# The adjacency in two tiles, p through DRAM by POOL's queue, and the scalings on ScalarE: a two-layer graph attention kernel on one core

## The chip, the cores and the metric

The kernel runs on one core of one Trainium2 chip. The metric is the device time of one execution in microseconds (us), the median of several runs. A core has five engines with an instruction stream each: TensorE (PE in the profile; PEld is its weight load), VectorE (DVE), ScalarE (ACT), GpSimd (POOL) and SyncE (SP). SP, ACT and POOL also issue DMA transfers, and each issues in its own order: an issue that waits holds up everything behind it on that engine. Instructions of one engine run in the order in which they were written; engines wait for each other by semaphores.

## The reference

There are 16 graphs of 1024 nodes with 256 features, x (16, 1024, 256), and an integer adjacency adj (16, 1024, 1024). In the data that the kernel is timed on, adj holds only 0 and 1 and is symmetric in its making.

```
# layer 0
e0    = leaky((h * a0) @ h.T)                  # slope 0.2; e1..e3 likewise for adj 2..4
alpha = sigmoid(where(adj == 1, e0, ..., -inf))
x1    = layernorm(x + alpha @ h + bias)
# layer 1
H  = x1 @ W;  s = H @ a_src;  d = H @ a_dst
e  = where(adj != 0, exp(-leaky(s[:, None] + d[None, :])), 0)
y  = elu((e @ H) / rowsum(e))
out = layernorm(x1 + y)
```

## The kernel before

All of it is float32 on the chip, except adj, which is kept as bfloat16. `one_kind_pass` computes everything for an adjacency of one kind (0 and 1); flags (`check_adj`, `check_pq`) collect whether that held, and only if one is raised `general_pass` runs afterwards. With this data it doesn't run.

P = 128, so a graph has NT = 8 blocks of 128 nodes, and HT = 4 blocks are a half. Each graph b passes through three stages, in which TensorE works almost without a gap. Stages of neighbouring graphs are interleaved by an order that is written out by hand in the loop `for b in range(1, B)`:

- **Strips of b** (lines 480 to 498). `strip(b, jt)` computes the scores of block jt with the blocks from jt on (they are symmetric, so only the upper triangle is computed): matmuls (L198), two tanh on ScalarE (L206, L207), the larger of both on VectorE (L208). The sigmoid is 0.5 (1 + tanh(z/2)). The scores lie in one of four `tb` tiles, so strip jt can be written only when strip jt-4 has been sent out. `finish` (L214) adds 1 and multiplies by adj, and POOL adds the identity, twice, to the diagonal block (L224), which puts the residual x into the sum. `dump` (L230, L234) turns the strip in blocks of 32 and sends it to DRAM by four DMAs, `gather` (L238) brings it back as the lower triangle, and `mask` (L244) multiplies that by adj. `project(b-1, t)` of the graph before runs between: matmuls of x1 with W and two further columns (L343), two exponentials into w and pq, and H scaled by w (L351 to L353). Since exp(-leaky(s+d)) is factored, layer 1 needs p, one number for each node, as a row on all 128 partitions. `spread_p` makes it at the stage's end: TensorE transposes each block's column, broadcast to 128 columns (L362, 8 per graph), and ScalarE copies the result from PSUM (L363).
- **Sum 0 of b** (lines 507 to 522): for each block t, `sum0` runs 8 matmuls (L294), VectorE takes the result with the bias (L302) and its mean and variance (L264, L265), and after four blocks POOL computes 1/sqrt of the variance (`rstd`, L271 to L279). `scale0` applies both on VectorE (L283). Beside it run the last masks, `weights(b-1, t)` (L375: the smaller of p times q and 1, masked by adj, 128x1024 at a time), `scale1` and the store of graph b-2, and on ScalarE `check_adj`, a square with a sum over 128x2048 of adj (L116).
- **Sum 1 of b-1** (lines 527 to 558): 8 times 8 matmuls of e with H and a column of ones (L382), `elu` (L397 to L403), `add` (L408, L409, mean and variance), and the preparation of the next graph: x1 goes to DRAM and comes back with its blocks of 32 turned (`save_x1`, `fetch_x1`, `turn_x1`, L320, L110, L331), and x of the next graph is loaded in the same form (`load_blocks`, `turn_x`).

The first graph has its own order (lines 439 to 470), with `mirror` (L252, L253) in place of dump, gather and mask; `make_Wx` prepares the further columns of W there, and x of graph 1 is loaded by ScalarE's DMA queue (line 451). The last graph has its own end (lines 561 to 599), in which the first three blocks of sum 1 run together, step by step with the weights.

adj of a graph is one tile [128, 8, 1024] with two buffers. [...]

Of the kernel before, what the change touches and what calls it, by code (L numbers as in the profile page):

```python
# [18 lines left out]
P = 128  # L19
# [10 lines left out]
def one_kind_pass(  # L30
# [60 lines left out]
    def load_adj(b, by_columns=False):  # L91
        adjs[b] = two.tile([P, NT, N], BF16, tag="adj", name=f"adj_{b}")
        rows = adjT[b].rearrange("(t p) i -> p t i", p=P)
        for h in range(2):
            for g in range(2):
                if by_columns:
                    v = (slice(None), ts(g, HT), ts(h, HALF))
                elif g == 0:
                    v = (slice(None), ts(h, HT))
                else:  # L100
                    continue
                nc.gpsimd.dma_start(adjs[b][v], rows[v])

    def load_blocks(dst, src, n0, n, queue=nc.sync):


        v = src[ds(n0, n), :].rearrange("(nb nn) (c q dd) -> q c nn nb dd", nn=SQ, c=ND, dd=SQ)
        for c in range(ND):
            for q in range(P // SQ):
                queue.dma_start(  # L110
                    dst[ts(q, SQ), c, ds(n0, n)].rearrange("p (nb dd) -> p nb dd", dd=SQ), v[q, c]
                )

    def check_adj(b, n):
        junk = one.tile([P, NT // CHECKS, N], BF16, tag="tmp", name=f"junk_{b}_{n}")
        nc.scalar.activation(  # L116
            junk,
            adjs[b][:, ts(n, NT // CHECKS), :],
# [20 lines left out]
    load_adj(0, by_columns=True)  # L139
    load_adj(1)  # L140
# [4 lines left out]
    a_bc = one.tile([P, 2 * D], F32, tag="p", name="a_bc")  # L145
# [64 lines left out]
    def finish(b, jt, c0=0, c1=N):  # L210
# [7 lines left out]
            adjs[b][:, jt, c0:c1],  # L218
# [23 lines left out]
    def mask(b, t):  # L242
        v = als[b][:, t + 1 :, ts(t, P)]
        nc.vector.scalar_tensor_tensor(v, v, 1.0, adjs[b][:, t + 1 :, ts(t, P)], ALU.add, ALU.mult)  # L244

    def mirror(b, t):

        for j0 in range(t + 1, NT, HT):
            n = min(HT, NT - j0)
            pt = ps_t.tile([P, HT, P], F32, tag="t", name=f"pal_{b}_{t}_{j0}")  # L250
            for q in range(n):
                nc.tensor.transpose(pt[:, q, :], tbs[b, t][:, ts(j0 + q - t, P)], ident)  # L252
            nc.vector.scalar_tensor_tensor(  # L253
                als[b][:, ds(j0, n), ts(t, P)],
                pt[:, 0:n, :],
                1.0,
                adjs[b][:, ds(j0, n), ts(t, P)],
                ALU.add,
                ALU.mult,
            )  # L260
# [21 lines left out]
    def scale(y, mv, r):  # L282
        nc.vector.tensor_scalar(y, y, mv[:, 0:1], r, ALU.subtract, ALU.mult)  # L283
# [3 lines left out]
    def sum0(b, t):  # L287
        if t == 0:
            x1s[b] = two.tile([P, NT, D], F32, tag="x1", name=f"x1_{b}")
            mv0s[b] = small.tile([P, NT, 2], F32, tag="mv0", name=f"mv0_{b}")  # L290
            r0s[b] = {}
# [12 lines left out]
        if t % HT == HT - 1:  # L304
            g = t // HT
            r0s[b][g] = rstd(mv0s[b][:, ts(g, HT), :], f"0_{b}_{g}")

    def scale0(b, t):
        scale(x1s[b][:, t, :], mv0s[b][:, t, :], r0s[b][t // HT][:, t % HT : t % HT + 1])
# [23 lines left out]
    def project(b, t):  # L333

        if t == 0:
            if b < B - 1:
                Hs[b] = one.tile([P, NT, D + 1], F32, tag="H", name=f"H_{b}")
            else:
                Hs[b] = two.tile([P, NT, D + 1], F32, tag="adj", name=f"H_{b}")
# [10 lines left out]
        w = Hs[b][:, t, D : D + 1]  # L350
        nc.scalar.activation(w, pt[:, 1:2], AF.Exp, scale=-SLOPE)  # L351
        nc.scalar.activation(pqs[b][:, t, :], pt[:, 0:2], AF.Exp, scale=SLOPE - 1.0)
        nc.scalar.mul(Hs[b][:, t, 0:D], pt[:, 2:], w)  # L353

    def spread_p(b, g):
# [7 lines left out]
        nc.scalar.copy(p_bcs[b][:, ts(g, HALF)], pt.rearrange("p t q -> p (t q)"))  # L363

# [6 lines left out]
    def weights(b, m):  # L371

        if m == 0:
            es[b] = one.tile([P, NT, N], F32, tag="ew" if b < B - 1 else "al", name=f"e_{b}")
        nc.vector.scalar_tensor_tensor(  # L375
            es[b][:, m, :], p_bcs[b], pqs[b][:, m, 1:2], adjs[b][:, m, :], ALU.mult, ALU.min
        )

    hs, ys, mv1s, r1s, rms = {}, {}, {}, {}, {}

    def sum1(b, t, acc, m):
# [3 lines left out]
            rhs=Hs[b][:, m, :],  # L385
# [26 lines left out]
    def center(b, t0, n):  # L412

        mv = mv1s[b][:, ds(t0, n), :]
        r = rstd(mv, f"1_{b}_{t0}")
        mr = small.tile([P, NT], F32, tag="mr", name=f"mr_{b}_{t0}")[:, 0:n]
        nc.gpsimd.tensor_tensor(mr, mv[:, :, 0], r, ALU.mult)
        nc.gpsimd.tensor_scalar(mr, mr, -1.0, None, ALU.mult)
        for t in range(n):
            rms[b, t0 + t] = r[:, t : t + 1], mr[:, t : t + 1]  # L420

    def scale1_act(b, t):
# [568 lines left out]
```

## Time and profile before

| | us |
|---|---|
| time, median of 3 runs (lowest to highest) | 1329.43 (1328.62 to 1329.67) |
| the profiled execution: its own time | 1330.3 |
| its span in the profile | 1328.4 |
| busy in the span: PE, DVE, ACT, POOL | 1280.3, 1019.5, 546.5, 243.4 |
| sum 0 stage of a graph, as a rule | 27.64 |
| sum 1 stage of a graph, as a rule | 27.84 |
| strips stage of graphs 2 to 15 | 23.54 to 27.39 |

In the groups of the profile a line gives engine and operation, the tiles written and read, the count, the busy time, the mean duration in ns, and the idle time of the engine just before these instructions with what ended it. In the table of waits each line is "engine line <- what it waited for: us in total, times, longest". In the timeline the columns are start, duration, engine, line, operation, and in brackets the idle time before. In the table of windows, an engine's busy time in the window is followed by its count of instructions; PEclk, DMA share and GB/s follow at the end.

### The profile page before, as it was taken

What the parts mean: (1) busy time and instruction counts of PE and PEld (TensorE: products, weight loads), DVE (VectorE), ACT (ScalarE), POOL (GpSimd) and SP (SyncE); (2) the same over time, 40 slices, a digit from 0 to 9 for tenths busy, and PEclk for the clock granted to TensorE, in tenths of its full rate; (3) what the DMA queues carried; (4) which work ended last, traced back from release to release, by engine and by line L of the source; (5) the groups of instructions that cost most, each with busy time, mean ns of one, the idle gap of its engine ahead of it and who ended that gap; (6) DMA issues with size and microseconds to landing.
All of it is one profiled execution on the core that took longest, in us unless ns stands there. A gap on an engine that the chain in (4) does not pass through costs nothing.

```text
span 1328.4 us, 17516 instructions
## 1 busy us (share of the span) xinstructions
PE 1280.3 (96%) x5550; PEld 1037.4 (78%) x5550; DVE 1019.5 (77%) x2318; ACT 546.5 (41%) x1236; POOL 243.4 (18%) x486
## 2 busy tenths in 40 slices
PE   7879999999999999999999999999999999999995
PEld 5758788687887878788687887878778687787874
DVE  5576886968869687886878869687886878869764
ACT  3352452715336162452715336162451624427034
POOL 2111111211112122111211112122111211112113
PEclk9999999999999999999999999999999999999998
DMA  9265687575677756687575677856686565775211
GB/s 215 54 133 113 109 174 143 113 164 104 145 141 157 160 103 150 109 180 143 111 162 106 150 138 152 162 105 151 111 177 130 110 151 106 172 143 111 68 29 66
DMA packets 606516, 173.36 MB, mean 130 GB/s; under 512 B 485584, under 2 KB 590928, under 8 KB 606416
## 3 DMA queue, kind: packets, MB, share of 16 engines
q1 hardware_dynamic: 580144, 137.56, 48.0%
q0 software_dynamic: 17952, 33.56, 14.8%
q10 hardware_dynamic: 8320, 1.05, 0.5%
q8 instruction: 46, 0.75, 0.2%
q14 instruction: 54, 0.44, 0.1%
HBM read 144.57 MB, written 61.08 MB: 155 GB/s over the span
## 4 chain that ended last, share of the span: by engine, by line
PE 83%; DVE 6%; DMA 3%; ACT 3%; SPq 2%; ACTq 1%; issue 1%; POOL 0%; DVEq 0%; POOLq 0%
PE acc L294 32%; PE acc L382 32%; PE pe L198 13%; PE pH L343 5%; DMA mir<-tb 2%; SPq L234 2%; DVE tb L208 1%; DVE al L214 1%; ACTq L110 1%; DVE tb L230 1%; ACT tb L206 1%; PE pp L362 1%; ACT low L207 1%; DVE st L264 1%; DVE y L409 0%
## 5 line engine op out<-in xcount | busy, mean ns | idle before, releaser
L382 PE MATMUL acc<-H,e 128*128 128x257 f32 x2048 | 448.7, 380 | 1.6 <-DVE e L375 1.6
L294 PE MATMUL acc<-x,al 128*128 128x256 f32 x2048 | 448.5, 381 | 0.0
L382 PEld LDWEIGHTS acc<-H,e 128*128 128x128 f32 x2048 | 387.9, 190 | 59.5 <-DVE e L375 2.4
L294 PEld LDWEIGHTS acc<-x,al 128*128 128x128 f32 x2048 | 389.5, 191 | 53.5 <-issue 0.5
L402 ACT ACTIVATE h<-acc,rinv 128x256 f32<-128x256 f32 x128 | 60.2, 470 | 562.2 <-DVE rinv L400 559.3
L198 PE MATMUL pe<-xa,xT 128*128 128x384 f32 (+3 forms) x768 | 269.4, 488 | 0.2 <-ACT low L207 0.2
L198 PEld LDWEIGHTS pe<-xa,xT 128*128 128x128 f32 x768 | 143.3, 191 | 87.5 <-issue 42.6
L271 POOL TENSOR_SCALAR ve<-mv 128x4 f32<-128x4 f32 (+3 forms) x51 | 18.0, 352 | 811.4 <-DVE mv L265 796.7
L375 DVE SCALAR_TENSOR_TENSOR e<-p,pq,adj 128x1024 f32<-128x1024 f32 x128 | 162.8, 1275 | 2.8 <-ACT p L363 2.8
L206 ACT ACTIVATE tb<-pe 128x512 f32<-128x512 f32 (+1 forms) x192 | 94.3, 491 | 136.5 <-PE pe L198 87.2
L343 PE MATMUL pH<-Wx,x1T 128*128 128x258 f32 x512 | 133.0, 386 | 7.1 <-DVE x1T L331 4.2
L343 PEld LDWEIGHTS pH<-Wx,x1T 128*128 128x128 f32 x512 | 97.2, 193 | 43.0 <-issue 17.6
L116 ACT ACTIVATE junk<-adj,minus 128x2048 bf16<-128x2048 bf16 x64 | 128.4, 2007 | 1.5
L397 DVE COPY rs<-acc 128x1 f32<-128x1 f32 x128 | 19.7, 154 | 138.9 <-PE acc L382 138.5
L208 DVE TENSOR_TENSOR tb<-tb,low 128x512 f32<-128x512 f32 (+1 forms) x192 | 99.3, 542 | 28.4 <-ACT low L207 25.8
L224 POOL TENSOR_TENSOR al<-ident,al 128x128 f32<-128x128 f32 x128 | 68.9, 538 | 240.9 <-DVE al L214 240.9
L214 DVE SCALAR_TENSOR_TENSOR al<-tb,adj 128x512 f32<-128x512 f32 (+7 forms) x132 | 99.4, 753 | 4.1
L302 DVE SCALAR_TENSOR_TENSOR x<-acc,bias_bc 128x256 f32<-128x256 f32 x128 | 54.3, 424 | 60.4 <-PE acc L294 59.2
L207 ACT ACTIVATE low<-pe 128x512 f32<-128x512 f32 (+1 forms) x192 | 93.3, 486 | 3.6 <-DVE tb L208 3.5
L273 POOL TENSOR_TENSOR r<-ve,power 128x4 f32<-128x4 f32 (+3 forms) x51 | 78.5, 1539 | 4.3
L230 DVE STREAM_TRANSPOSE tb<-tb 128x896 f32<-128x896 f32 (+6 forms) x105 | 74.7, 712 | 3.6
L244 DVE SCALAR_TENSOR_TENSOR al<-al,adj 128x896 f32<-128x896 f32 (+6 forms) x105 | 72.9, 694 | 0.9 <-DMA al<-mir 0.7
(58 smaller groups left out, 866.3 us busy)
## 6 DMA issues: line engine op xcount, KB each, us to landing
adj<-in_adjT POOLq DMA_DIRECT2D x30, 1024.0 KB, 13.6
x_rows<-x SPq DMA_DIRECT2D x32, 512.0 KB, 3.7
x1T<-x_rows SPq DMA_DIRECT2D x256, 64.0 KB, 2.4
x<-in_x SPq DMA_DIRECT2D x15, 1024.0 KB, 6.2
out<-y SPq DMA_DIRECT2D x30, 512.0 KB, 3.0
xT<-in_x SPq DMA_DIRECT2D x112, 128.0 KB, 3.2
mir<-tb SPq DMA_DIRECT2D x60, 112.0 KB, 2.4
al<-mir SPq DMA_DIRECT2D x15, 448.0 KB, 4.1
```

The source lines that it names most:

```text
L116: nc.scalar.activation(junk, adjs[b][:, ts(n, NT // CHECKS), :], AF.Square, bias=minus1, scale=2.0, accum_out=chk[:, b * CHECKS + n : b * ...
L198: nc.tensor.matmul(pe[:, 0:w], lhsT=xTs[b][:, c, ts(jt, P)], rhs=xas[b][:, c, ds(jt * P + o, w)], start=(c == 0), stop=(c == ND - 1),)
L206: nc.scalar.activation(tb[:, ds(o, w)], pe[:, 0:w], AF.Tanh, scale=0.5)
L207: nc.scalar.activation(low[:, 0:w], pe[:, 0:w], AF.Tanh, scale=0.5 * SLOPE)
L208: nc.vector.tensor_tensor(tb[:, ds(o, w)], tb[:, ds(o, w)], low[:, 0:w], ALU.max)
L214: nc.vector.scalar_tensor_tensor(als[b][:, jt, c0:c1], tbs[b, jt][:, c0 - jt * P : c1 - jt * P], 1.0, adjs[b][:, jt, c0:c1], ALU.add, ALU. ...
L230: nc.vector.transpose(tb, tb)
L273: nc.gpsimd.tensor_tensor(r, ve, power[:, 0:n_t], ALU.pow)
L294: nc.tensor.matmul(acc, lhsT=als[b][:, jt, ts(t, P)], rhs=xs[b][:, jt, :], start=(jt == 0), stop=(jt == NT - 1),)
L343: nc.tensor.matmul(pt, lhsT=x1Ts[b][:, c, ts(t, P)], rhs=Wx[:, c, :], start=(c == 0), stop=(c == ND - 1),)
L375: nc.vector.scalar_tensor_tensor(es[b][:, m, :], p_bcs[b], pqs[b][:, m, 1:2], adjs[b][:, m, :], ALU.mult, ALU.min)
L382: nc.tensor.matmul(acc, lhsT=es[b][:, m, ts(t, P)], rhs=Hs[b][:, m, :], start=(m == 0), stop=(m == NT - 1),)
```

## The change

- adj of a graph becomes two tiles of four row blocks each (`adj0`, `adj1`, two buffers each). The first half of graph b+1 is loaded at t = 5 of the sum 0 stage, when the weights of blocks 0 to 3 have been made, the second after the stage. Instructions on adj that cross the border of the halves are split in two (`adj_rows`).
- p: TensorE transposes the eight columns at once to 8 rows, ScalarE copies 8x128, POOL's queue writes that to DRAM and reads it back to all 128 partitions (`share_p`). This is issued at the strips' step 6 (step 7 for the first graph) and no longer at the stage's end; the projections come earlier in the stage. The weights are made from t = 2 of sum 0 on, not from t = 0. The last graph keeps `spread_p`.
- `scale0` and `scale1` run on ScalarE, from factors that POOL makes (`center`).
- The first graph: `make_Wx` after the first four strips; x of graph 1 by SP's queue; `check_adj(0, t)` at t = 0 to 3 rather than 4 to 7. Graph 1's strips get another order for x1 of graph 0.
- The end: weights of block 2 before the loop over m, and in the last loop the elu of a block stands before the add of the block before it.

```diff
+    def load_adj(b, g, columns=None):
+        if (b, g) not in adjs:
+            adjs[b, g] = two.tile([P, HT, N], BF16, tag=f"adj{g}", name=f"adj_{b}_{g}")
+        columns = columns or slice(None)
+        rows = adjT[b].rearrange("(t p) i -> p t i", p=P)[:, ts(g, HT), columns]
+        nc.gpsimd.dma_start(adjs[b, g][:, :, columns], rows)
+
+    def adj_rows(b, j0, j1, columns):
+        for g in range(2):
+            k0, k1 = max(j0, g * HT), min(j1, (g + 1) * HT)
+            if k0 < k1:
+                yield slice(k0, k1), adjs[b, g][:, k0 - g * HT : k1 - g * HT, columns]
...
     def mask(b, t):
-        v = als[b][:, t + 1 :, ts(t, P)]
-        nc.vector.scalar_tensor_tensor(v, v, 1.0, adjs[b][:, t + 1 :, ts(t, P)], ALU.add, ALU.mult)
+        for js, rows in adj_rows(b, t + 1, NT, ts(t, P)):
+            v = als[b][:, js, ts(t, P)]
+            nc.vector.scalar_tensor_tensor(v, v, 1.0, rows, ALU.add, ALU.mult)
...
-    def scale(y, mv, r):
-        nc.vector.tensor_scalar(y, y, mv[:, 0:1], r, ALU.subtract, ALU.mult)
+    def center(mv, what):
+        r = rstd(mv, what)
+        n = mv.shape[1]
+        mr = small.tile([P, NT], F32, tag="mr", name=f"mr_{what}")[:, 0:n]
+        nc.gpsimd.tensor_tensor(mr, mv[:, :, 0], r, ALU.mult)
+        nc.gpsimd.tensor_scalar(mr, mr, -1.0, None, ALU.mult)
+        return [(r[:, t : t + 1], mr[:, t : t + 1]) for t in range(n)]
+
+    def scale(y, r, mr):
+        nc.scalar.activation(y, y, AF.Identity, bias=mr, scale=r)
...
+    def share_p(b):
+        pt = ps_t.tile([P, HT, P], F32, tag="t", name=f"prow_{b}")[0:NT, 0, :]
+        nc.tensor.transpose(pt, pqs[b][:, :, 0], ident)
+        row = small.tile([NT, P], F32, tag="row", name=f"row_{b}")
+        nc.scalar.copy(row, pt)
+        p_row = dram.tile([N], F32, tag="p_row", name=f"p_row_{b}")
+        nc.gpsimd.dma_start(p_row.rearrange("(t p) -> t p", p=P), row)
+        p_bcs[b] = one.tile([P, N], F32, tag="p", name=f"p_{b}")
+        nc.gpsimd.dma_start(p_bcs[b], p_row.partition_broadcast(P))
...
-    make_Wx()
     strip(0, 0)
...
+    make_Wx()
     load_x(1)
     new_xT(1)
-    load_blocks(xTs[1], x[1], 0, N, nc.scalar)
+    load_blocks(xTs[1], x[1], 0, N)
...
-        if t >= NT - CHECKS:
-            check_adj(0, t - NT + CHECKS)
+        if t < CHECKS:
+            check_adj(0, t)
...
-        projects = [[jt] for jt in range(NT)]
+        projects = [[0, 1], [2], [3], [4, 5], [6], [7], [], []]
         if prev == 0:
-            projects = [[], [], [], [0, 1], [2, 3], [], [4, 5], [6, 7]]
+            projects = [[], [], [], [], [0, 1], [2, 3], [], [4, 5, 6, 7]]
...
-            if prev == 0 and jt in (1, 2):
-                scale0(0, 2 * jt + 2)
-                scale0(0, 2 * jt + 3)
-            if prev == 0 and jt == 2:
+            if prev == 0 and jt == 1:
+                for t in range(HT, NT):
+                    scale0(0, t)
                 save_x1(0, 1)
-                fetch_x1(0, 1)
-            if prev == 0 and jt in (2, 5):
-                turn_x1(0, (jt - 2) // 3)
             finish(b, jt)
             if jt < NT - 1:
                 dump(b, jt)
+            if prev == 0 and jt == 1:
+                fetch_x1(0, 1)
+            if prev == 0 and jt in (3, 6):
+                turn_x1(0, (jt - 3) // 3)
             if jt >= 1:
                 gather(b, jt - 1)
             for t in projects[jt]:
                 project(prev, t)
+            if jt == (6 if prev > 0 else 7):
+                share_p(prev)
             if jt >= 5:
                 mask(b, jt - 5)
-        for g in range(2):
-            spread_p(prev, g)
...
-            weights(prev, t)
+            for m in ([], [], [0, 1], [2], [3], [4], [5], [6, 7])[t]:
+                weights(prev, m)
...
             sum0(b, t)
+            if t == 5 and not last:
+                load_adj(b + 1, 0)
...
         if not last:
-            load_adj(b + 1)
+            load_adj(b + 1, 1)
...
     for m in range(NT):
-        if m >= 2:
+        if m >= 3:
             weights(last, m)
-        if m == 3:
+        if m == 5:
             add(done, NT - 1)
-            center(done, 0, NT)
+            r1s[done] = center(mv1s[done], f"1_{done}")
...
         elu(last, t, acc)
+        if 1 <= t < NT - 1:
+            add(last, t - 1)
+        if t == 6:
+            add(last, t)
         if t in (3, 6):
-            center(last, t - 3, 3)
-        add(last, t)
+            r1s[last] += center(mv1s[last][:, ds(t - 3, 3), :], f"1_{last}_{t - 3}")
+        if t == 7:
+            add(last, t)
```

## The prediction

> **What bounds the kernel now.** I read the shares of busy time first, then the chain that ended last, then windows over the three stages of each graph, then who waits for whom, then the timeline of a slow and of a fast strips stage.
>
> ```profile
> PE 1280.3 (96%) x5550; PEld 1037.4 (78%) x5550; DVE 1019.5 (77%) x2318; ACT 546.5 (41%) x1236; POOL 243.4 (18%) x486
> ```
>
> TensorE is the bound; a change is worth what it takes from TensorE's own instructions or from its 48 us of idle time. The windows (in order: sum 0, sum 1, strips of the next graph, twice) say where those lie:
>
> ```profile
> 338.17:365.81 27.64, 27.64 (x130) 24.33 (x129) 23.79 (x50) 9.31 (x11) 3.98 (x7) 1.00 0.60 139
> 365.81:393.65 27.84, 27.84 (x130) 24.27 (x129) 17.36 (x55) 7.95 (x16) 3.64 (x8) 1.00 0.86 162
> 393.65:417.23 23.58, 23.57 (x90) 15.69 (x89) 22.05 (x39) 16.26 (x51) 7.18 (x13) 1.00 0.57 114
> 576.15:603.79 27.64, 27.64 (x130) 24.33 (x129) 24.57 (x52) 9.31 (x11) 3.86 (x7) 1.00 0.63 142
> 603.79:631.63 27.84, 27.84 (x130) 24.27 (x129) 17.14 (x55) 7.95 (x16) 3.64 (x8) 1.00 0.86 162
> 631.63:656.92 25.29, 23.56 (x90) 15.69 (x89) 23.28 (x41) 16.22 (x51) 7.18 (x13) 1.00 0.55 108
> ```
>
> Both sums are solid TensorE work. Only the strips stage varies: the 14 of graphs 2 to 15 take 345.86 us together for 331.49 us of TensorE work, so 14.37 us idle. (One of them and the sum 0 before it ran at a lower granted clock, 1.7 us each; I leave that in on both sides.) The waits name the rest:
>
> ```profile
> ACT tb L206 <- DMA mir<-tb: 25.4, 17, 3.2
> PE pp L362 <- ACT pq L352: 14.6, 12, 2.2
> ACT tb L206 <- DMA xT<-in_x: 13.6, 1, 13.6
> PE pal L252 <- DVE tb L208: 3.5, 1, 3.5
> ```
>
> The slow stage's end in the timeline, TensorE, then ScalarE, then VectorE:
>
> ```profile
> 653.95 0.93 PE L362 MATMUL pp<-ident,pq 128*128 128x128 f32 x7
> 656.60 0.32 PE L362 MATMUL pp<-ident,pq 128*128 128x128 f32 x1 [1.73 <-ACT pq L352]
> 656.76 5.58 PE L294 MATMUL acc<-x,al 128*128 128x256 f32 x25
> ```
> ```profile
> 655.97 0.28 ACT L206 ACTIVATE tb<-pe 128x128 f32<-128x128 f32 x1 [1.51 <-DMA mir<-tb]
> ```
> ```profile
> 652.68 1.08 DVE L244 SCALAR_TENSOR_TENSOR al<-al,adj 128x896 f32<-128x896 f32 x1
> ```
>
> The last of the eight transposes of p needs pq of block 7; ScalarE makes that only after the tanh of strip 7, which waits until strip 3 has left its tile by DMA. So p stands between strips and sum 0 with its own 1.07 us (0.93 and the last 0.14) and with a DMA's lateness. Mask 0, which sum 0 needs as well, was done at 653.76, before.
>
> **The change, part by part.** All times are against the profiled execution (1330.3 us, span 1328.4), which lies 0.9 above the median of 1329.43.
>
> *p, graphs 1 to 14.* Taken away: 8 transposes by 0.134 us = 1.07 a graph. Added: one of 0.13. Over 14 strips stages that is 15.0 - 1.9 = 13.1 us. The wait goes too: the row needs pq 7, now projected at step 5, before strip 6; nothing in front of it on ScalarE waits for a late DMA. If the whole 14.37 goes, the stage is 22.6 us, and 27.5 us are won. What is late next? With the projections earlier TensorE finishes strips 1 to 3 one projection (0.87) later and strips 4 and 5 two (1.74). VectorE follows: in the fast stage it began strip 4's maximum at 411.19 after a wait for ScalarE, so at 412.9 now; finish and turn take 1.4, strip 5 (maximum, finish, turn 0.55 + 0.56 + 0.45) ends at 416.55. Mask 0 is now 384 and 512 wide instead of 896; by the rows of those widths 0.53 + 0.66 for 1.08. The first half ends at 417.1. TensorE would be through at 393.65 + 22.6 = 416.25, takes the one matmul of sum 0 that needs no mask until 416.7, and waits 0.4. The second half is done at 417.75, before its matmul at 418.4. So I set the stage at 23.0; 14 by 0.4 = 5.6, and the gain is 27.5 - 5.6 = **21.9 us**. Ends: 27.5 with no wait, 8 with every stage at 24.0 (whole mask waited for). Mask 1 ends some 2.4 us behind mask 0, for a sum at 3.45 behind: hidden.
>
> *p's way through DRAM.* On POOL the write stands behind the diagonal of strip 6, some 2.5 us after sum 0's start S; the read waits there for the write. Queued behind them: the diagonal of strip 7 (needed at S + 27) and `center` at S + 14: both hidden. No row shows a small DMA of this queue. From below: the 16 KB write of the mirror, 1.9 us, the 448 KB gather 4.1, with issues of 0.8 each = 7.6. From above: the shortest adj load of POOL's queue, 8.6 us (1 MB out of 2 MB), twice, with issues = 18.8. I take 7.6, since both sizes lie by the SP rows; a broadcast costs no more than a plain load (a_bc 256 KB 7.7 us, Wx 256 KB 9.3 us, issued side by side). p lands at S + 10.1. The weights of t = 2 come up on VectorE at S + 8.7 and wait 1.4 us. That is covered: three accumulators let TensorE run to block 5 (S + 17.3) before it needs block 2 taken away. VectorE then has eight weights (10.2), five evictions of 1.1 and masks 0.7 left = 16.4, and the last weight is due at S + 27.64 + 3.0 = 30.6. So p may land until S + 14.2: cover of 4.1 us.
>
> [...] The row: POOL's diagonal of 0.456 us took 1.08 us beside VectorE at 97.04, so POOL is slowed by one VectorE instruction. An estimate by that: two issues, about 1.3 us later, inside the cover. [...]
>
> *Scalings.* VectorE loses 240 instructions of about 0.4, ScalarE gains them by 0.54 to 0.60. In sum 0 VectorE loses 8 + 4 of them, 4.9 of 24 us. ScalarE had 9.3 of 27.64 busy there and gets 7: hidden. POOL gains two of 0.2 for each `center`, beside 0.23 us of diagonal work it is idle: hidden. Against p's lateness this is VectorE's reserve.
>
> *adj in halves.* Moving the load beside sum 0 takes DMA share from sum 1 (0.86) to sum 0 (0.60). No instruction of graphs 1 to 15 waited for adj: nothing won. The issue on POOL waits for weight 3, done a step before; behind it stands only `center` of block 7. The three split masks add about 0.12 each to VectorE, counted above.
>
> *The first graph.* ScalarE issued eight DMAs of x for graph 1 from 23.07 to 37.2 and could not compute; that is the 13.6 us of the waits, and TensorE lost 3.54 at `mirror` and about 1.0 in the next sums. On SP, behind only loads already issued, nothing waits behind them until x1's save at 58. Won 4.5; the split mirrors (three on the path, 0.13) cost 0.4; the earlier start of VectorE without `make_Wx` is taken back by ScalarE, which delivers strip 1 only at 17.7: 0.2. Sum 4.3. `make_Wx` (2.9) falls into VectorE's 2.8 us idle at 26.5: at most 0.3 late. Graph 1's strips took 33.8 us from the end of sum 0. ScalarE began them 4.4 late, behind two `check_adj` that are gone now; VectorE can start 2.5 earlier. But the four scalings hold ScalarE for 2.3 at step 1, SP's fetch of x1 now stands in front of gather 0 (so mask 0 and dump 2 wait for 4 us of issues), and four projections stand at the end. My chain (second x1 half turned at 27, four projections 3.5, row 31.5) gives 31.6, so 2.2 won; between 6 (the start's 2.5 and half the idle time) and -3 (the fetch's 4 us arriving whole). Both together **6.5 us**.
>
> *The end.* VectorE spent 2.99 us a block from 1296.0 on, 0.99 of it waiting for ScalarE's exponential; with elu before the previous add it needs 2.0, less than TensorE's 3.48, so the last elu follows the last matmul at 1313.7. The adds of 5 and 6 end at 1312.2 and 1313.7, the last at 1317.0. POOL then becomes the bound: `center` of three blocks 3.2, two of one block 2.8 each, one after another = 1321.0, for 1322.84 before. **1.9 us**.
>
> Sum: 21.9 + 6.5 + 1.9 = 30.3. 1330.3 - 30.3 = 1300.0 for an execution like the profiled one, 1299.1 from the median. I say 1300.
>
> **The rivals.**
>
> 1. *VectorE becomes the bound of the strips stage.* For it: it is busy 22 to 23.3 of the stage before already. If it runs 1 us later than in my chain, the stage is 24.0, the gain 8 + 8.4 = 16: 1313. Against: in the fast stage it still waited 0.53 for ScalarE.
> 2. *p comes late* (the other side). For it: two DMAs one after another in a queue of which the profile shows only large transfers, beside gather, x and xT. Every us beyond S + 14.2 costs 15 us over the 15 graphs. From 2.0 us beyond it (13.8 us for both DMAs in place of 7.6) the whole gain is gone. At the upper end of 18.8 us, 7 beyond, it would be 1300 + 105 = 1405; half way beyond the cover (3.5 by 15 = 52), 1352. Against: small transfers land in 1.9 to 4.1 here.
> 3. *Nothing is won but the transposes.* Another dump or gather takes the place of the wait, and the 14.37 us of idle time stay: 13.1 + 8.4 gives 1309. Against: mask 0's gather landed 2 to 4 us ahead.
> 4. *The first graph's new order loses* 3 us instead of winning 2.2: 1305.
>
> **How the numbers follow.** Forecast (1292 to 1306) 0.60; rival 1 0.12, rival 2 0.10, rival 3 0.10, rival 4 0.08. The measurement tells about 0.2% (2.7 us) from no change. Faster is all but rival 2 and a little of rival 1's tail: 0.87; same 0.03; slower 0.10. The low end, 1290, is no wait at mask 0 (5.6) and half of graph 1's further gain; the high end, 1317, takes in rivals 1 and 3 and leaves out rival 2.
>
> **What would show it.** Right: the L362 line has 8 instructions instead of 128, strips windows of 22.6 to 23.3, TensorE waiting at sum 0 for L244 (mask) by under 0.5; a wait of VectorE's weights for the p DMA of 1 to 3 us; the wait for xT gone. Wrong: strips windows over 24; sum 1 windows over 27.84 with TensorE waiting for the weights, or sum 0 windows over 27.64.

## The result, and the profile after

The changed kernel takes 1307.46 us (median of 4 runs, 1303.62 to 1307.63), the kernel before beside it 1329.55 us (1328.62 to 1332.45). The ratio is 0.983, with a 95% interval of 0.981 to 0.984. So it is faster by 22 us, or 1.7%; the forecast was 1300 us, so 7.5 us of the expected 30 are missing. The profiled execution took 1307.63 us, with a span of 1305.8 us against 1328.4 us before.

Shares of busy time and three stages of the changed kernel (window, its length, busy time of TensorE, its weight load, VectorE, ScalarE and POOL, then granted clock, DMA share, GB/s; in order sum 0, sum 1 and the strips of the next graph):

```profile
PE 1268.1 (97%) x5445; PEld 1024.2 (78%) x5445; DVE 941.3 (72%) x2126; ACT 652.5 (50%) x1461; POOL 304.2 (23%) x608
```
```profile
329.33:357.60 28.27, 27.90 (x130) 24.24 (x129) 23.14 (x48) 11.84 (x21) 7.75 (x14) 1.00 0.84 178
357.60:385.44 27.84, 27.84 (x129) 24.28 (x128) 16.37 (x52) 12.99 (x25) 3.30 (x9) 1.00 0.75 155
385.44:408.02 22.58, 22.58 (x82) 14.89 (x81) 19.28 (x33) 15.76 (x48) 7.53 (x13) 1.00 0.52 103
```

The strips of graphs 2 to 15 are now all 22.58 us and solid TensorE work, where they were 23.54 to 25.79 (27.39 in the table of before, where a half-clock window of a sum 0 was counted to the strips). In exchange each of their sums 0 is 28.27 us, 0.63 us more than before. The table of waits names what does that, among others (engine, line, what it waited for: us in total, times, longest):

```profile
POOL p L397 <- DMA p_row<-row: 40.3, 15, 4.6
ACT y L437 <- DMA out<-y: 19.4, 12, 2.5
DVE e L409 <- DMA p<-p_row: 17.2, 15, 2.8
PEld acc L312 <- DVE al L252: 10.8, 14, 0.8
PE acc L312 <- DVE al L252: 5.2, 14, 0.4
PE pH L365 <- DVE x1T L349: 4.3, 1, 4.3
PE pH L365 <- DMA mir<-tb: 3.1, 1, 3.1
```

Mask 0 (L252) holds the start of 14 sums 0. The weights (L409) wait for p in graphs 0 to 14, and nothing on TensorE waits for these weights; its only waits for L409, 1.4 us, are in the last graph, which keeps the transposes. A wait that I had not forecast is that of ScalarE's exponential (L437): `y` has one buffer, and it waits until the graph before has been stored from it. The start of a sum 0, at 408.02, in the timeline of TensorE, of POOL and of VectorE:

```profile
408.02 0.60 PE L312 MATMUL acc<-x,al 128*128 128x256 f32 x2
408.39 1.15 DVE L252 SCALAR_TENSOR_TENSOR al<-al,adj 128x384 f32<-128x384 f32 x2
408.99 16.24 PE L312 MATMUL acc<-x,al 128*128 128x256 f32 x74 [0.37 <-DVE al L252]
410.81 0.64 POOL L395 DMA_DIRECT2D p_row<-row  x1
413.46 0.56 POOL L397 DMA_DIRECT2D p<-p_row  x1 [2.01 <-DMA p_row<-row]
418.36 2.48 DVE L409 SCALAR_TENSOR_TENSOR e<-p,pq,adj 128x1024 f32<-128x1024 f32 x2 [1.05 <-DMA p<-p_row]
```

The span in pieces, each cut at the start of a stage in TensorE's timeline or at the last scaling:

| piece | before | after | difference | forecast |
|---|---|---|---|---|
| up to graph 1's strips | 63.57 | 58.29 | -5.28 | -4.3 |
| graph 1's strips | 33.65 | 35.56 | +1.91 | -2.2 |
| from there to the last sum 1 | 1150.22 | 1129.33 | -20.89 | -21.9 |
| the last sum 1 to TensorE's last matmul | 66.74 | 66.53 | -0.21 | 0 |
| from there to the end of the last scaling | 9.29 | 7.91 | -1.38 | -1.9 |
| the last scaling to the span's end | 4.93 | 8.18 | +3.25 | 0 |
| sum | 1328.40 | 1305.80 | -22.60 | -30.3 |

The large term came as forecast. The 7.7 us that are missing lie at two places: graph 1's strips (4.1) and what follows the last scaling (3.25); the other differences nearly cancel.

In graph 1's strips TensorE ran at half clock for a part of the time. Windows of the changed kernel there, cut every 3.41 us from 75.72, which nearly fits the changes of the granted clock at 75.64, 79.05, 85.88 and 92.70 us (columns as above):

```profile
72.00:75.72 3.72, 0.00 (x1) 0.00 (x1) 3.65 (x7) 0.64 (x2) 0.45 (x1) 0.99 0.90 141
75.72:79.13 3.41, 3.41 (x8) 2.76 (x9) 1.79 (x3) 0.68 (x3) 0.46 (x1) 0.51 0.82 169
79.13:82.54 3.41, 3.41 (x15) 2.60 (x15) 0.92 (x2) 2.34 (x10) 0.00 (x0) 1.00 1.03 210
82.54:85.96 3.42, 1.16 (x8) 0.89 (x6) 3.32 (x8) 1.67 (x7) 0.91 (x2) 0.99 0.98 211
85.96:89.37 3.41, 2.61 (x6) 2.18 (x7) 3.07 (x7) 0.52 (x3) 0.45 (x1) 0.50 0.88 172
89.37:92.78 3.41, 3.41 (x9) 2.67 (x9) 0.00 (x0) 1.33 (x7) 0.00 (x0) 0.51 0.49 109
```

Behind a window with no matmul work, and again behind one with 1.16 us of it, a window at half clock follows (0.51 and 0.50), in the second case two. Cut at the changes themselves, the three stretches are 3.41 us at a granted clock of 0.50, 6.83 us at 1.00 and 6.82 us at 0.50.

In the kernel before, there were three such windows (from 38.70, 79.66 and 977.36 us, each of 3.41 us at 0.50), the last of them in a sum 0 of a late graph (29.33 us for 27.64); that 1.69 us is part of the 20.89.

The end shows on POOL's queue, in the instructions of the line of the closing `If` and in the DRAIN of the kernel's last line behind them (durations in ns: shortest, median, longest; then first and last start in us). First before, then after:

```profile
L952 POOLq EVENT_SEMAPHORE  x5: 17/43/43, 1325.7 to 1326.0; - x5
L952 POOLq COMPARE_BRANCH  x1: 45/45/45, 1323.1 to 1323.1; - x1
L952 POOLq INC_SWDGE_SEM  x1: 400/400/400, 1326.1 to 1326.1; - x1
L987 POOLq DRAIN  x3: 40/107/894, 1326.5 to 1328.2; - x3
```
```profile
L982 POOLq EVENT_SEMAPHORE  x5: 17/43/43, 1300.0 to 1302.4; - x5
L982 POOLq COMPARE_BRANCH  x1: 45/45/45, 1297.3 to 1297.3; - x1
L982 POOLq INC_SWDGE_SEM  x1: 632/632/632, 1302.5 to 1302.5; - x1
L1017 POOLq DRAIN  x3: 46/107/1865, 1303.1 to 1305.6; - x3
```

From the branch to the start of INC_SWDGE_SEM POOL's queue takes 3.0 us before and 5.2 us after. The difference lies among the five semaphore instructions: from the first to the last of them it is 0.3 us before and 2.4 us after. INC_SWDGE_SEM is 0.23 us longer and the longest DRAIN 0.97 us. Together these make about the 3.25 us.

### The profile page after: what moved, and what is told of

It reads as the page before. It is cut to its first block, busy times and chain, and to the rows that moved or that the text cites. A ratio compares the mean times of both kernels' runs of the same rounds, so it can differ in the third digit from the quotient of the medians.

```text
span 1305.8 us, 17594 instructions
## 1 busy us (share of the span) xinstructions
PE 1268.1 (97%) x5445; PEld 1024.2 (78%) x5445; DVE 941.3 (72%) x2126; ACT 652.5 (50%) x1461; POOL 304.2 (23%) x608
## 5 line engine op out<-in xcount | busy, mean ns | idle before, releaser
L301 ACT ACTIVATE x<-x,mr,r 128x256 f32<-128x256 f32 x128 | 69.2, 592 | 231.4 <-POOL mr L297 231.4
L409 DVE SCALAR_TENSOR_TENSOR e<-p,pq,adj 128x1024 f32<-128x1024 f32 x128 | 159.7, 1270 | 20.1 <-DMA p<-p_row 17.2
L365 PEld LDWEIGHTS pH<-Wx,x1T 128*128 128x128 f32 x512 | 100.4, 197 | 45.2 <-issue 14.0
L231 POOL TENSOR_TENSOR al<-ident,al 128x128 f32<-128x128 f32 x128 | 60.0, 472 | 212.3 <-DVE al L221 212.1
L320 DVE SCALAR_TENSOR_TENSOR x<-acc,bias_bc 128x256 f32<-128x256 f32 x128 | 54.0, 422 | 62.4 <-PE acc L312 62.2
```

The lines of the kernel that those rows point to most:

```text
L365: nc.tensor.matmul(pt, lhsT=x1Ts[b][:, c, ts(t, P)], rhs=Wx[:, c, :], start=(c == 0), stop=(c == ND - 1),)
L409: nc.vector.scalar_tensor_tensor(es[b][:, m, :], p_bcs[b], pqs[b][:, m, 1:2], adjs[b, m // HT][:, m % HT, :], ALU.mult, ALU.min)
```

## The experiments

Twelve kernels ran in three sets, each on one chip with runs of the kernel before beside it: 1328.26 us (e1, e2, e3, e7), 1328.27 us (e4, e5, e6, e8) and 1334.72 us (e9, e11, e12, e13). Beside the third set the kernel before was 6 us slower, while e9 and e13 lie where the first two sets put them; so I compare that set by its own members and by stages. Stages are cut as in the table above.

### e1: only p's new way, on the kernel before

```diff
-        projects = [[jt] for jt in range(NT)]
+        projects = [[0, 1], [2], [3], [4, 5], [6], [7], [], []]
...
+            if jt == (6 if prev > 0 else 7):
+                share_p(prev)
...
-        for g in range(2):
-            spread_p(prev, g)
...
-            weights(prev, t)
+            for m in ([], [], [0, 1], [2], [3], [4], [5], [6, 7])[t]:
+                weights(prev, m)
```

> The kernel before with the new way of p alone (one transpose, the row through DRAM by POOL's queue, projections earlier, weights from t = 2); adj in one tile, scalings on VectorE, first graph and end as before. If p's wait at the end of the strips is what was removed, the stages of graphs 2 to 15 shorten as in the changed kernel (some 20 us in all) and start and end stay: about 1309 us. If VectorE's relief from the scalings is needed as well, or the adjacency's earlier load, it stays above 1320.

Measured: 1318.52 us, ratio 0.993 (0.991 to 0.994). The strips fell to the same 22.58 us, but sum 0 rose to 28.80 us, 1.16 us over that of before. With adj in one tile, mask 0 is one instruction of 896 columns, and sum 0 waits for all of it:

```profile
PE acc L294 <- DVE al L244: 12.7, 14, 0.9
```

So the two-piece mask, a side effect of the halves of adj, is worth 28.80 - 28.27 = 0.53 us a graph, 7.4 us over 14 graphs: sum 0 can start on the first piece. The expectation of 1309 left that out. (Scalings and the earlier load of adj, in which e1 differs as well, have no part in it: with either undone, in e7 and e8, sum 0 stays at 28.27 us.)

### e2: the changed kernel with p as before

```diff
-        projects = [[0, 1], [2], [3], [4, 5], [6], [7], [], []]
+        projects = [[jt] for jt in range(NT)]
...
-            if jt == (6 if prev > 0 else 7):
-                share_p(prev)
...
+        for g in range(2):
+            spread_p(prev, g)
...
-            for m in ([], [], [0, 1], [2], [3], [4], [5], [6, 7])[t]:
-                weights(prev, m)
+            weights(prev, t)
```

> The changed kernel with p as before (eight transposes at the end of the strips, projections one per step, weights from t = 0); all else as changed. If p carries the gain: about 1327 us, with strips stages of 23.5 to 25.5 us and TensorE again waiting for pq of block 7. If scalings and adj carry it: about 1310.

Measured: 1322.43 us, ratio 0.995 (0.993 to 0.997). Strips of 23.36 to 25.43 us, sums 0 of 27.64 us, and TensorE's wait of before is back:

```profile
PE pp L384 <- ACT pq L374: 12.4, 11, 1.9
```

p's part is worth 15.0 us in the presence of the rest, 9.7 us without it (e1). The remainder alone gives 6 us. The expectation of 1327, which has no sum, was 4.6 us too high; 2.6 us of that are the end, which here is 80.05 us from the last sum 1's start against 82.62 us in the changed kernel.

### e3: the eight transposes kept, at the new place

```diff
             if jt == (6 if prev > 0 else 7):
-                share_p(prev)
+                for g in range(2):
+                    spread_p(prev, g)
```

> The changed kernel, but p made by the eight transposes and two copies of before, at the new place (step 6 of the strips), so no DRAM. It tells the place from the transposes' own time. If the wait behind pq of block 7 was the larger part: TensorE spends 0.94 us a stage more on transposes, but its wait for mask 0 (0.37 to 0.63) goes under them, so 0.3 to 0.6 us a graph, 1312 to 1316 us. If the transposes' time counts in full and nothing hides: 1321. If moving it keeps the wait: above 1325.

Measured: 1305.45 us, ratio 0.983 (0.981 to 0.984): no slower than the changed kernel. That was the largest surprise. The strips are 23.34 us, 0.76 us longer by the transposes, but sum 0 is 27.63 us and waits for no mask, since TensorE now comes 0.76 us later to it. Together 50.97 us against 50.85 us. So what gave nearly all of the 20 us was the new order, and the DRAM way added 0.12 us a graph: it took 0.76 us from TensorE only to make it wait 0.63 us for mask 0. These 1.7 us over 14 graphs are less than the closing costs more with it (8.2 us from the last scaling to the span's end, 5.0 us here). The order is three things, the earlier projections, the place in front of strip 7 and the weights from t = 2 on; no run moves one of them alone.

### e4, e5: p later by one and by two hops through DRAM

```diff
         nc.gpsimd.dma_start(p_row.rearrange("(t p) -> t p", p=P), row)
+        for k in range(1):          # e5: range(2)
+            hop = dram.tile([N], F32, tag=f"hop{k}", name=f"hop_{k}_{b}")
+            nc.gpsimd.dma_start(hop.rearrange("(t p) -> t p", p=P), p_row.rearrange("(t p) -> t p", p=P))
+            p_row = hop
```

> The changed kernel with one more copy of p's row from DRAM to DRAM on POOL's queue, so that p lands later by one small DMA with its issue and wait, some 3.3 us: at S + 13.6 in place of S + 10.3. The prediction's cover ends at S + 14.2 (14.8 with the wait at mask 0): VectorE waits longer for p, TensorE not at all, and the time stays at 1304 to 1309 us. If p's path is already the bound, 3.3 us for each of 15 graphs: 1357.

> The same with two more copies: p lands at about S + 17, 2.2 to 2.8 us beyond the cover. By the prediction's sum 15 graphs lose that each: 1340 to 1350 us, with TensorE waiting for the weights at the start of sum 1 or for an eviction in sum 0. If the cover is much wider than I reckoned: 1308.

Measured: e4 1322.89 us, ratio 0.994 (0.992 to 0.996), so 15 us lost where I had expected none; e5 1383.36 us, ratio 1.041 (1.039 to 1.043), 76 us lost. The first weights start 9.5 to 11.5 us after sum 0's start in the changed kernel, 12.6 to 15.2 us after it in e4 and 14.8 to 19.3 us in e5. In e4 strips and sums 0 stay as they were, but for 0.3 us in one sum 0, and five sums 1 of fourteen are long (33.94, 28.45, 28.3, 35.17 and 30.7 us for 27.84), yet not by the weights. Of the 17.4 us that these five have too much, 12.2 us are waits for the exponential and 5.1 us half clock behind them (behind the first, the mean granted clock from 214.00 to 217.50 us is 0.73). TensorE's waits of e4:

```profile
PE acc L420 <- ACT y L441: 12.2, 5, 4.9
PE acc L312 <- DVE al L252: 5.2, 14, 0.4
PE acc L420 <- DVE e L413: 1.4, 2, 0.9
```

The timeline of e4 at the first long one, SP, ScalarE, POOL and TensorE:

```profile
199.34 1.09 ACT L301 ACTIVATE x<-x,mr,r 128x256 f32<-128x256 f32 x2 [20.98 <-POOL mr L297]
...
205.78 0.58 ACT L301 ACTIVATE y<-y,mr,r 128x256 f32<-128x256 f32 x1
206.39 0.38 SPq L455 DMA_DIRECT2D out<-y  x1
206.42 0.85 POOL L97 DMA_DIRECT2D adj<-in_adjT  x1
...
214.74 0.47 ACT L441 ACTIVATE y<-acc,rinv 128x256 f32<-128x256 f32 x1 [6.03 <-DMA out<-y]
...
215.27 19.35 PE L420 MATMUL acc<-H,e 128*128 128x257 f32 x80 [4.16 <-ACT y L441]
```

Late weights make VectorE's statistics and with them POOL's factors late; ScalarE waits for those at 199.34 with the first scaling of x1, and behind it in ScalarE's order stand the scalings of the graph two before. Its store goes out at 206.39, together with the second half of adj. The next sum's exponential needs that `y` free until 214.7. In the changed kernel the same store went out at 200.09 and the exponential followed at 206.41, in time for TensorE.

In e5 TensorE waits at two places:

```profile
PE acc L312 <- DVE x L320: 31.4, 14, 4.1
PE acc L420 <- ACT y L441: 24.4, 10, 5.9
```

The larger wait is in sum 0, and is the one that the prediction had named: TensorE stands before block 5, because VectorE takes block 2 away (L320) only behind the first weights. All sums 0 together are 44.7 us longer than in the changed kernel (31.4 us of waits, 10 us half clock), the sums 1 33.5 us (24.4 us of waits behind y's store, 8.5 us half clock). The mean granted clock of the profiled execution is 0.980, where it is 0.992 in the changed kernel.

### e13: the late p of e4, with the store of y brought forward

```diff
-            if done >= 0:
-                scale1(done, t)
-                if t in (3, 7):
-                    store(done, t - 3, HT)
+            if done >= 0 and t < HT:
+                scale1(done, 2 * t)
+                scale1(done, 2 * t + 1)
+                if t in (1, 3):
+                    store(done, 2 * t - 2, HT)
```

> The run with one more hop through DRAM on p's way (1322.9 us), with the scalings of the graph two before and their two stores brought forward: two a tile in sum 0's tiles 0 to 3, the stores after tiles 1 and 3 in place of 3 and 7. Theory: a later p does not reach TensorE by the weights, but makes the statistics of graph b-1 and with them ScalarE's first scalings late, behind which the scalings of graph b-2 and the store of its y are queued; the next sum's elu waits for that store (5 waits of TensorE, 4.9 us in the mean, on y). With the store early those waits go: 1307.5 to 1309. The rival: the weights themselves, or the order on VectorE behind them, make sum 1 late; then it stays at 1320 to 1323.

Measured: 1307.52 us (1305.46 to 1309.13), 15 us less than e4. All sums 1 are 27.84 us again, and the wait of ScalarE for `out` is gone from the table, although the weights come as late as in e4: 12.8 to 15.1 us after sum 0's start. So e4's loss came by the store of y and the scalings in front of it, as the theory says, and TensorE's own cover reaches to some 15 us: of the sums 0 only the one whose weights start at 15.05 us is longer, 28.38 us for 28.27. (The five waits on y in e4 are 4.9 us at the longest, not in the mean as I wrote; the mean is 2.4 us.)

### e6: graph 1's strips in the order of before

```diff
-            projects = [[], [], [], [], [0, 1], [2, 3], [], [4, 5, 6, 7]]
+            projects = [[], [], [], [0, 1], [2, 3], [], [4, 5], [6, 7]]
...
-            if prev == 0 and jt == 1:
-                for t in range(HT, NT):
-                    scale0(0, t)
+            if prev == 0 and jt in (1, 2):
+                scale0(0, 2 * jt + 2)
+                scale0(0, 2 * jt + 3)
+            if prev == 0 and jt == 2:
                 save_x1(0, 1)
+                fetch_x1(0, 1)
+            if prev == 0 and jt in (2, 5):
+                turn_x1(0, (jt - 2) // 3)
...
-            if prev == 0 and jt == 1:
-                fetch_x1(0, 1)
-            if prev == 0 and jt in (3, 6):
-                turn_x1(0, (jt - 3) // 3)
```

> The changed kernel with graph 1's strips in the order of before (scalings at steps 1 and 2, x1's second half saved and fetched at step 2, projections at steps 3, 4, 6, 7). In the changed kernel this stage takes 35.6 us, and its last four projections ran at half clock. If the new order is what costs there, the stage comes back to 30 to 34 and the time to 1303 to 1306; if the clock drops whatever the order, no change within 2 us.

Measured: 1303.00 us (1302.66 to 1303.44), 4.5 us below the changed kernel. Graph 1's strips take 31.21 us. First the changed kernel's stage, then that of e6 (columns as above; clock near the end):

```profile
58.29:93.85 35.56, 27.86 (x83) 17.97 (x81) 23.31 (x39) 17.62 (x53) 6.61 (x16) 0.86 0.70 140
```
```profile
57.74:88.95 31.21, 24.93 (x82) 15.71 (x81) 22.39 (x36) 17.26 (x53) 6.30 (x16) 0.95 0.62 126
```

Of the 4.35 us, 2.93 us are TensorE's busy time, that is the clock, and 1.42 us idle time. The size varies from run to run: the stage takes 34.15 to 36.42 us in the kernels of this study with the new order, and 31.21 to 33.15 us in e6, e11 and e12, which have the old one.

### e7, e8: the scalings on VectorE; both halves of adj after sum 0

```diff
-    def scale(y, r, mr):
-        nc.scalar.activation(y, y, AF.Identity, bias=mr, scale=r)
+    def scale(y, r, mr, act=False):      # e7; True in the end's last loop and behind it
+        if act:
+            nc.scalar.activation(y, y, AF.Identity, bias=mr, scale=r)
+        else:
+            nc.vector.tensor_scalar(y, y, r, mr, ALU.mult, ALU.add)
```
```diff
-            if t == 5 and not last:
-                load_adj(b + 1, 0)
...
         if not last:
+            load_adj(b + 1, 0)
             load_adj(b + 1, 1)
```

> The changed kernel with the scalings of the stages back on VectorE (the same form, two scalars for each block; the last two graphs' output scalings stay on ScalarE as before). By the prediction's sum the last weight then comes 3.5 us later on VectorE, at about S + 30.2, and is due at S + 30.6: 1307 to 1310 us. If VectorE is then the bound of sum 0: 1 to 3 us a graph, 1322 to 1350, with TensorE waiting for the weights at the start of sum 1.

> The changed kernel with the first half of adj loaded after sum 0, right before the second, as the whole was before. If the earlier load is worth nothing (no instruction waited for adj): 1307 us and unchanged stages. If it relieved the transfers beside sum 1: 1311 or more, with sum 1 over 27.84.

Measured: e7 1306.29 us, e8 1305.07 us; in both every stage of graphs 2 to 15 has the length that it has in the changed kernel (22.58, 28.27, 27.84). Neither part gains there. What little they lie below 1307.46 us is in the closing, 6.3 and 6.4 us in place of 8.2 us, and in e8 also in graph 1's strips (34.15 us; in e7 they are longer, 36.42 us).

### e9: the end in the order of before

```diff
-            if last and t == 7:
-                weights(b, 2)
...
-        if m >= 3:
+        if m >= 2:
...
-        if m == 5:
+        if m == 3:
...
-        if 1 <= t < NT - 1:
-            add(last, t - 1)
-        if t == 6:
-            add(last, t)
...
-        if t == 7:
-            add(last, t)
+        add(last, t)
```

> The changed kernel with the end in the order of before (three tiles of the last graph's weights built at the start of its sum, statistics of the last tile in one go). By the prediction's term 1.9 us are lost against the changed kernel's 1307.5: 1309.4; by the two traces (end of TensorE's work to the last scaling 9.29 us before, 7.91 us after) 1.4 us: 1308.9. The rival: the closing of POOL's queue after the last scaling, 8.18 us in the changed kernel's profile against 4.93 us before, took the gain back, and its length hangs on when POOL's last work ends; then the old end costs nothing: 1306 to 1307.5. What tells them apart beside the time is the stretch from the last scaling to the span's end: 8 us by the first, 5 us by the rival.

Measured: 1308.66 us (1305.48 to 1309.34). TensorE's last matmul starts at 1289.41 and the last scaling ends at 1298.72, 9.31 us later, where it was 7.91 us. From there to the span's end it is 8.18 us. So the new end is worth 1.4 us, as the two traces said, and the order of the end has no part in the long closing.

### e11: mask 0 earlier, and graph 1's old order

```diff
-            if jt >= 5:
+            if jt == 3 and prev > 0:
+                mask(b, 0)
+            if jt >= (6 if prev > 0 else 5):
                 mask(b, jt - 5)
```

(and the diff of e6)

> The changed kernel with mask 0 moved from step 5 of the strips to the end of step 3, where VectorE has an idle stretch, and with graph 1's row transposes and projections in the order of before. Theory: each sum 0 of graphs 2 to 15 loses 0.62 us to mask 0 (28.27 us against 27.65 us where nothing waits), so 14 x 0.62 = 8.7 us go, and graph 1's strips give back 4.4 us, as its order of before did alone (31.21 us against 35.56 us): 1307.5 - 13.1 = 1294. The rival: VectorE is the bound there, so that an earlier mask only makes a later one late, or the strips' own finishing steps: strips grow by 0.3 to 0.6 us and the time stays at 1303, which is graph 1's part alone.

Measured: 1295.09 us (1294.85 to 1297.14), ratio 0.970 (0.969 to 0.972), the fastest kernel of this study and 13.6 us below e9 on the same chip. Its windows of one strips stage and the sum 0 behind it:

```profile
402.19:429.82 27.63, 27.63 (x130) 24.33 (x129) 22.18 (x46) 12.00 (x21) 7.80 (x14) 1.00 0.86 189
379.61:402.19 22.58, 22.58 (x82) 14.89 (x81) 20.32 (x35) 15.75 (x48) 7.51 (x13) 1.00 0.52 102
```

Both are now solid TensorE work, 50.21 us together for 50.85 us. All fourteen sums 0 are 27.63 us and no strips stage grew: VectorE had the room, and the wait was one of order. The part of the 0.63 us that had not shown as a wait (0.26) went with it.

### e12: e11 with the transposes in place of the DRAM way

The diff against e11 is that of e3 against the changed kernel.

> The run with mask 0 early and graph 1's old order, but with p spread by TensorE's broadcast transposes at the new place in place of the way through DRAM. With mask 0 in step 5 the two ways differed by 0.12 us a graph (strips and sum 0 together 50.85 us with DRAM, 50.97 us with transposes), because the DRAM way only reached the wait for mask 0 sooner. Theory: with that wait gone the transposes' 0.76 us (strips 23.34 us against 22.58 us) show whole, 14 x 0.74 = 10.4 us, of which the closing without p's transfers on POOL's queue gives back some 3 us (79.5 us from the last sum's start against 82.6 us): 1294 + 10.4 - 3 = 1301. The rival: the way through DRAM is worth nothing wherever mask 0 stands; then this run is within 2 us of the one with the DRAM way.

Measured: 1303.33 us (1302.93 to 1304.67), 8.2 us slower than e11. Strips of 23.34 us and sums 0 of 27.63 us, 50.97 us together, just as in e3: moving mask 0 gave the transposes nothing, as they had already hidden it. 14 times 0.76 = 10.6 us are the transposes; graph 1's strips add 1.4 us (33.15 against 31.75 us), graph 0 is 0.6 us shorter, and the end gives 3.4 us back (4.86 us from the last scaling to the span's end against 8.3 us): 8.0 us, as the spans have it (1301.1 and 1293.1). So the DRAM way is worth 0.76 us a graph once mask 0 is out of its way, and 0.12 us while it is not.

## Why the prediction was right, and where it failed

**What bounds the kernel: right.** The wait for the eighth transpose was the loss. It comes back in e2, with p's old place and the old order of projections and weights.

**p, graphs 1 to 14 (21.9 us): nearly right in size, with some luck, and wrong in what earns it.** Measured 20.9 us, and 1.69 us of it are luck: a half-clock window in a late sum 0 of the profiled execution before that did not come again and that the forecast had left in on both sides. (I wrote that two stages had lost 1.7 us each, and it was one.) That leaves 19.2 us. The wait of 0.4 us at mask 0 was 0.37 us, but cost 0.63 us: the first matmul behind it starts 0.53 us later than in e11, which has no such wait, and takes 0.48 us for 0.38. Strips and sum 0 together are 50.85 us, where the forecast had 23.0 and 27.64, so 0.2 us a graph or 3 us over 14 graphs are missing. I had also named sums 0 over 27.64 us as a sign of being wrong; they came, because my sum had put the wait into the strips stage. The step "taken away: 8 transposes, 13.1 us" failed as an account: with the transposes kept (e3) the time is no longer. The two effects were not additive, because the 0.94 us that I took from TensorE (0.76 us at the new place) went into waiting for the mask. I had both numbers, 1.07 us and 0.4 us, in one chain, and did not ask what the stage would be with the transposes kept at the new place.

**p's way through DRAM: the landing right, the cover right for TensorE, the consumer missed.** Write 2.7 us, read 4.2 us and issues of 0.64 and 0.56 us; the first weights started at S + 10.34 in the stage shown, for 10.1 forecast. TensorE's deadline of S + 14.2 was near: e13's weights start at up to S + 15.1 at no loss in sum 1. It is set by block 2's eviction in sum 0, though, not by the last weight at sum 1, for which TensorE waits in none of the graphs 0 to 14 even in e5. The price of 15 us per us came out for this path: e5 lies 3 us beyond S + 14.2 in the median graph, which gives 45 us, and its sums 0 are 44.7 us longer, though 10 us of that are half clock, which the price did not include. But e5 lost 76 us: the sums 1 add 33.5 us, 24.4 us of them TensorE's waits for the exponential behind y's store. That is the missed step: I asked who waits for the late weights, and stopped at TensorE. The late statistics hold ScalarE, whose order has the previous graph's store behind them; with the store where the change has it, the cover was under 4.1 us: 3 us more already cost 15 us (e4).

**POOL slowed by VectorE**: no run here shows a delay of p by it. In the changed kernel the two issues took 0.64 to 0.65 and 0.55 to 0.56 us in all 15 graphs, for 0.8 each in the forecast, and in the stage shown p lands 0.24 us behind the sum that did without such a delay, where the estimate had 1.3 us.

**Scalings and adj halves hidden: right** (e7, e8). But I counted the split of mask 0 as a small cost, while its use, sum 0 starting on the first piece, sat unnamed inside the stage of 23.0 us. It is worth 0.53 us a graph (e1).

**The first graph: graph 0 right (5.3 us for 4.3), graph 1 wrong.** The step that failed is "my chain gives 31.6, so 2.2 won"; the stage grew by 1.9 us. Rival 4 came true, by a mechanism that I had named: the fetch of x1 stands before gather 0 on SP, so dump 2 went out late, VectorE waited 4 us for its tile, and turned the second half of x1 that much later. The changed kernel's timeline of SP and VectorE:

```profile
72.11 4.26 SPq L112 DMA_DIRECT2D x1T<-x_rows  x8
76.47 0.43 SPq L245 DMA_DIRECT2D al<-mir  x1
77.01 3.14 SPq L241 DMA_DIRECT2D mir<-tb  x4
...
81.58 0.56 DVE L215 TENSOR_TENSOR tb<-tb,low 128x384 f32<-128x384 f32 x1 [4.00 <-DMA mir<-tb]
...
85.35 1.20 DVE L349 STREAM_TRANSPOSE x1T<-x1T 128x1024 f32<-128x1024 f32 x1
86.76 6.65 PE L365 MATMUL pH<-Wx,x1T 128*128 128x258 f32 x16 [3.06 <-DMA mir<-tb]
```

Then the clock doubled the price: the last four projections took 6.65 us, nearly all of it at a granted clock of 0.50 (85.88 to 92.70 us), which I had set at 3.5. With the order of before the same stage takes 31.21 us (e6), so the start's gain was there and the new order threw it away. So the order alone costs 4.35 us between these two profiles.

**The end: 1.4 us for 1.9 (e9). What follows the last scaling was missing from the sum**, and grew by 3.25 us. Every run with p's transfers on POOL's queue has a longer closing than the runs without them (6.0 us at least against at most 5.02); why some take 2 us more than that is open, see the last section.

**The rivals.** Rival 1 (VectorE the bound) did not occur; e11 shows that VectorE had room for mask 0 earlier. Rival 2 (p late) did not occur, but stood nearer than I had priced it. Rival 3 (only the transposes won) is the reverse of what e3 shows; its 1309 us lies nearer to the measured time than my 1300, so it is the stages and not the time that tell them apart. Rival 4 occurred, and with the closing it makes the difference between 1300 and 1307.

## What to carry to other kernels

When an operation is moved and replaced in one change, cost the move with the old operation still in place: here the place earned nearly all, and the replacement paid only once the next wait (mask 0) was moved too. When a result comes late, follow every engine behind it to the end of its order, to single-buffered tiles and their stores above all; the first consumer had the cover that I worked out and a later one did not. A wait of TensorE can cost more than its own length: in the traces of before and after, from 12 us on, each wait that left 1.24 us of matmul work or less in a window of 3.41 us was followed by one or two such windows at a granted clock of 0.50, and one of these made a sum 0 1.69 us longer. So a few long waits can be worth more than the table of waits says, and the granted clock of the windows behind them shows it.

## What the runs showed of the hardware that I had not expected

- **A wait of 1.88 us was followed by half clock, and a later one of 3.31 us by full clock (e6).** Behind the first, eight projection matmuls took 3.44 us (the granted clock is 0.50 from 72 to 74 us), where the next eight took 1.91 us. Behind the second, eight took 1.98 us, at 1.00. By e6's windows of 1 us each, an estimate puts its half clock from 71.36 to 74.78 us; in windows of that length the first wait leaves 1.53 us of matmul work in one, and the second is spread over two, which keep 2.08 and 1.44 us. The traces of before and after, from 12 us on up to the last matmul, divide into such windows at the changes of the granted clock. There five at full clock with 1.24 us of matmul work or less (0.46, 0.00 and 1.17 in before, 0.00 and 1.24 in after) were followed by 0.50. The next higher ones, 1.43, 1.63 and 1.78 us in before, were followed by 1.00, so beside the 1.53 us of e6 the matmul work in the window before does not tell alone what follows. Of the windows at half clock, the one with 2.53 us (after) was followed by another, and those with 2.84 us (before), 3.32 us (after) and 3.41 us (both) by full clock. What sets the clock is not shown by these runs. TensorE's timeline of e6:

```profile
70.96 3.44 PE L365 MATMUL pH<-Wx,x1T 128*128 128x258 f32 x8 [1.88 <-DVE x1T L349]
...
76.21 1.91 PE L365 MATMUL pH<-Wx,x1T 128*128 128x258 f32 x8
...
83.58 1.98 PE L365 MATMUL pH<-Wx,x1T 128*128 128x258 f32 x8 [3.31 <-issue]
```

- **The closing was longer in the runs with p's transfers on POOL's queue, but not in the order of their number.** The time from the last scaling to the span's end was 4.86 to 5.02 us without them in graphs 0 to 14 (before, e2, e3, e12). With two a graph it was 6.04 to 6.44 us in e1, e7 and e8, and 8.14 to 8.30 us in the changed kernel, e6, e9 and e11, with three (e4, e13) 6.59 and 6.81 us, with four (e5) 7.37 us. INC_SWDGE_SEM took 0.400 us in the kernel before and 0.632 us in the changed one, the DRAIN behind it 0.894 and 1.865 us. In the changed kernel there is a gap of 2.1 us in front of the third of POOL's five semaphore instructions, which the kernel before does not have. What POOL waits for there is not settled; it may have a part in the one of four runs of the changed kernel that took 1303.62 us.
